# A graph layer with a highway gate: the root rows come by plain gathers and VectorE adds, and the last group of edges begins one product sooner

## The chip, the cores and the metric

The kernel runs on one core of a Trainium2 chip. Times are device microseconds. The core has five engines that run side by side, each in the order of its own instruction stream: TensorE (PE in the profile, its weight loads PEld), VectorE (DVE), ScalarE (ACT), GpSimd (POOL) and SyncE (SP). Large contiguous loads and stores are issued from SP; every gather and scatter by row indices is issued from POOL. Sixteen DMA engines carry out both.

## The reference

There are 1250 nodes with 1024 features in fp32, 20000 directed edges sorted by their destination, and 8 edge types. Cut to what matters:

```python
h = maximum(layernorm(x), 0)
u = h @ root + bias
for r in range(8):
    mask = (edge_type == r)
    sums = segment_sum(h[src] * mask[:, None], dst, 1250)
    cnt  = segment_sum(mask, dst, 1250)
    u = u + (sums / maximum(cnt, 1)[:, None]) @ weight[r]
z = concatenate([u, h], axis=1) @ w_gate + b_gate
out = x + tanh(u) * z + h * (1 - z)
```

## The kernel before

**The matrices.** The kernel multiplies h by ten 1024 x 1024 matrices and u by an eleventh, in fp32, numbered s: s = 0 to 7 are the eight edge types' weights, s = 8 is `root`, s = 9 (`LAST`) is the lower half of `w_gate` (for h), and s = 10 (`NM - 1`) is its upper half (for u). Products with s = 0 and s = 10 run over five pairs of 128-row blocks (`product`, seven batches of matmuls each, with a call `between(j)` after each batch). Products with s = 1 to 9 are cut by a fast scheme into seven smaller products n = 0 to 6 (function `kind`), written (s, n) here. Each (s, n) has five calls, `call(0)` to `call(4)`, at which work for the other engines is put into their streams; `at_call` holds where the program stands. In `kind`, L487 and L506 add a product's inner part (`ys`) in PSUM for the even and the odd blocks, `inner_sums` (L315 to L327) forms sums of quarters of the weights (the right sums) and of h (the left sums), and `to_rows_of` (L416 to L437) adds results into rows. `inner_sums` for the next product is emitted by `next_sums`, right after `call(2)`. Left sums that `LOADED` names for (s, n) are loaded from DRAM instead of made.

**The rows.** The products with s = 0 to 7 are stored as rows to `y[g]`, in three groups of edge types (g = 0, 1, 2, the types from `R0[g]` on), h times `root` to `hr_dram`, and s = 9 to `z_dram`.

**The edges.** While the products run, DVE and POOL build an index (`columns`, `positions`, `nodes_in_order`): for each group, nodes sorted by their number of edges, and for each node up to `SLOTS` rows of `y[g]` to add. This index work is a generator, one step at a call; the calls in `FULL_CALLS` get none, and the few small matmuls in it wait for a chosen call (`while at_call[2] != 2`).

`edges(g, to, late, more, lag, ring, seq)` then adds up a group. For each of the ten blocks of sorted nodes there is an accumulator u (128 x 1024). `first_u` reads it from `u_dram[g - 1]` by a gather (for g = 0 it is the bias). Then come `K[g][d]` slots: `slot_row` (L1446) gathers one row of `y[g]` for each of 128 nodes into the next of five buffers `got`, and `add_slot` (L1457) multiplies it by a weight and adds it to u on DVE. One slot is one step of the generator. For groups 0 and 1 the block is scattered to `u_dram[g]` behind its last slot (L777). For the last group (`LG`, g = 2) blocks come in the order `SEQ` and stay in SBUF as `us[d]`; there the rows of `hr_dram` are added as well, by `add_hr` (through `rows_of`, L766), an indirect DMA that adds what it gathers to u on the way: for the blocks from the third on, four steps ahead of the block's first slot, and for the first two (`HR_LATER`) after call (9, 0, 3). The accumulators of the fifth to the ninth block lie in parts of `h_all` that stage 9 no longer needs (`U_LATER`).

**Pacing.** `spread(e, total, of)` gives the steps of a group to the calls: each call of (s, n) counts `SHARE[n]` parts, each call of a gate product (s = 10) counts `GATE` parts, and after each call so many steps have been made as the counted parts ask for. Group 0 runs from (3, 1) to (6, 1), group 1 from there to (9, 0), and the last group from (9, 0) to the end of the third gate product; the borders are `CHANGE`. Between group 1 and the last group the program finishes the rows of the product before (`rest()`), stores what is held (`store_rows()`), and passes a branch on the register `far` (L1818) that is not taken here.

**The gate.** A gate product i uses blocks 2i and 2i + 1 of `SEQ`: their u is turned (`gate_turned`, transposes L571, copies L576, sums L609) and put through tanh (`gate_h`) during the product before, and z and h rows are gathered with an add (`gate_z`, `gate_d`).

Of the kernel before, what the change touches and what calls it, by code (L numbers as in the profile page):

```python
# [15 lines left out]
OP = mybir.AluOpType  # L16
# [5 lines left out]
def tile_rgcn_highway(  # L22
# [31 lines left out]
    nc = tc.nc  # L54
# [11 lines left out]
    ND = -(-N // P)  # L66
    NP = ND // 2
    NCH = 160
    FULL = E // NCH
    G = 3  # L70
    R0 = (0, 3, 6, R)
    K = ((21, 10, 8, 7, 7, 6, 5, 5, 4, 3), (21, 10, 8, 7, 7, 6, 5, 5, 4, 3),
         (17, 7, 6, 5, 4, 4, 3, 3, 2, 2))
    LAST = R + 1
    CALLS = 5
    BEGIN = (3, 1)
    WAIT1 = 3
    FULL_CALLS = [(4, k) for k in range(5)] + [(n, 3) for n in range(7)]
    CHANGE = ((6, 1), (9, 0))
    SEQ = (4, 5, 6, 7, 8, 9, 2, 3, 0, 1)  # L80
    REGULAR = {9: (5,)}
    LOADED = {7: (0, 1, 2, 3, 4, 5), 8: (0, 1, 2, 3, 4, 6), 9: (0, 2, 3, 4)}
    SHARE = (9, 11, 9, 11, 9, 11, 10)
    GATE = 15
    U_LATER = range(4, 9)
    HR_LATER = 2
    SLOTS = 22
    NCNT = SLOTS + 2
    STEP = 8
# [11 lines left out]
    GOT = 5  # L101
    UB = 4
    LATE = 4
# [8 lines left out]
    def nrows(d):  # L112
        return min(P, N - d * P)
# [13 lines left out]
    hr_dram = dram.tile([N, D], F32, name="hr_dram")  # L127
# [587 lines left out]
    NM = len(mats)  # L715
    fac = [Factors(w) for w in mats]

    at_call = [0, 0, 0]
# [98 lines left out]
    def nodes_in_order(pos, ids_f, room, many):  # L817

        parts = []
        for g in range(G):  # L820
            a, b, small = room(g)
            a = a[:, :KEYS].rearrange("p (c q) -> p c q", q=P)
            b = b[:, :2 * ND * ND].rearrange("p (c d) -> p c d", d=2 * ND)
            hi_i, lo, hi, block, lo_f = [small[:, k * ND:(k + 1) * ND] for k in range(5)]
            hi_i, lo, hi = hi_i.bitcast(I32), lo.bitcast(I16)[:, :ND], hi.bitcast(I16)[:, :ND]
            at = pos[:, g * ND:(g + 1) * ND]
            nc.vector.tensor_copy(block, many[:, :ND])
            nc.vector.tensor_copy(hi_i, at)
            nc.vector.tensor_single_scalar(hi_i, hi_i, 7, op=OP.arith_shift_right)
            nc.vector.tensor_copy(hi, hi_i)  # L830
            nc.vector.scalar_tensor_tensor(lo, hi_i, float(-P), at, op0=OP.mult, op1=OP.add)
            nc.vector.tensor_tensor(a, lo[:, :, None].to_broadcast([P, ND, P]),
                                    many[:, None, :].to_broadcast([P, ND, P]), op=OP.is_equal)
            yield
            nc.vector.tensor_tensor(b[:, :, :ND], hi[:, :, None].to_broadcast([P, ND, ND]),
                                    many[:, None, :ND].to_broadcast([P, ND, ND]), op=OP.is_equal)
            nc.vector.tensor_tensor(b[:, :, ND:], b[:, :, :ND],
                                    block[:, :, None].to_broadcast([P, ND, ND]), op=OP.mult)
            nc.vector.tensor_scalar(b[:, :, :ND], b[:, :, :ND], ids_f[:, :1], None, op0=OP.mult)
            parts.append((a, b, lo_f))  # L840
        while at_call[2] != 2:
            yield
        p = sum_bank("ps_q")[:, :2 * G * ND].rearrange("p (g d) -> p g d", g=G)
        for g, (a, b, lo_f) in enumerate(parts):
            for c in range(ND):
                nc.tensor.matmul(p[:, g], a[:, c], b[:, c], start=(c == 0), stop=(c == ND - 1))
        for g, (a, b, lo_f) in enumerate(parts):
            nc.vector.tensor_copy(lo_f, p[:, g, :ND])
            nc.vector.scalar_tensor_tensor(node[:, g, :], p[:, g, ND:], float(P), lo_f,
                                           op0=OP.mult, op1=OP.add)  # L850
            nc.vector.scalar_tensor_tensor(node_key[:, g, :], lo_f, float(ND), p[:, g, ND:],
                                           op0=OP.mult, op1=OP.add)
            if g:
                nc.vector.tensor_single_scalar(node_key[:, g, :], node_key[:, g, :], g * KEYS,
                                               op=OP.add)
        for g in range(G):
            for d in range(ND):
                rows_of(idx[:, g, d, :], table_rows, node_key[:, g, d:d + 1])
            yield
# [44 lines left out]
    def positions(runs, pos, ids_f, room):  # L904
# [50 lines left out]
        nc.vector.reduce_sum(first.rearrange("p g d -> p (g d)")[:, :, None],  # L955
                             pairs.rearrange("p g d e -> p (g d) e"), axis=AX.X)
        yield
        while at_call[2] != 2:
            yield
        p = sum_bank("ps_q")  # L960
        for k, t in enumerate((above, ones)):
# [30 lines left out]
    with ExitStack() as early:  # L992
# [20 lines left out]
        class Normed:  # L1013
# [13 lines left out]
            def spread(self):  # L1027
                n = self.n
                nc.vector.bn_aggr(self.mv[:n], self.st[:n].rearrange("p a b -> p (a b)"))
                nc.scalar.activation(self.sd[:n], self.mv[:n, 1:2], AF.Sqrt, bias=eps[:n])  # L1030
# [383 lines left out]
    with ExitStack() as edges_part:  # L1414
# [7 lines left out]
        def got():  # L1422
            t = gpool.tile([P, D], F32, name="got")
            if fresh[0]:
                nc.vector.memset(t, 0.0)
                fresh[0] -= 1
            return t
# [24 lines left out]
        def add_slot(u, g, d, k, at, w, t=None):  # L1452
            n = nrows(d)
            if t is None:
                t = slot_row(g, d, k, at)
            w = w[:n, d, k:k + 1]
            nc.vector.scalar_tensor_tensor(u[:n], t[:n], w, u[:n], op0=OP.mult, op1=OP.add)  # L1457

        us = {}

        def new_u(q, g=0):

# [12 lines left out]
                rows_of(u[:n], u_dram[g - 1][:, :], node[:n, g, d:d + 1])  # L1475
            return u

        def edges(g, to, late=0, more={}, lag=GOT, ring=True, seq=range(ND)):

            places = range(ND)
            starts = [late + sum(K[g][d] for d in seq[:q]) for q in range(ND + 1)]
            leaves = [starts[q + 1] - 1 + lag for q in places]
            reads = [max(-1, starts[q] - (9 if q in more else 5),
                         leaves[q - UB] if ring and q >= UB else -1,
                         starts[UB - 1] - 4 if not ring and q >= UB else -1) for q in places]
            u, then, early = {}, {}, []
            reads[0] = late - 3  # L1490
            for t in range(-1, leaves[-1] + 4):
                if 0 <= t < LATE:
                    early.append(slot_row(g, seq[0], t, idx[:, g]))
                for q, d in enumerate(seq):
                    if starts[q] <= t < starts[q + 1]:
                        add_slot(u[q], g, d, t - starts[q], idx[:, g], w_of[:, g],
                                 early.pop(0) if early else None)
                for q, d in enumerate(seq):
                    if t == leaves[q]:
                        then[t + 3] = to(q, d, u[q])  # L1500
                if then.get(t):
                    then[t]()
                for q, d in enumerate(seq):
                    if t == reads[q]:
                        u[q] = first_u(g, q, d)
                    if q in more and t == starts[q] - 4:
                        more[q](d, u[q])
                yield

        def u_back(g):  # L1510
# [25 lines left out]
        def kinds(first, end):  # L1536

            return [(a, b) for a in range(first[0], NM) for b in range(7 if a <= LAST else NP)
                    if first <= (a, b) < end]
# [269 lines left out]
        late = LATE  # L1809
# [35 lines left out]
                    p.next()  # L1845


        LG = G - 1
        def add_hr(d, u):
            n = nrows(d)  # L1850
            rows_of(u[:n], hr_dram[:, :], node[:n, LG, d:d + 1], OP.add)

        def place_of(what, i, part):

            o = ("z", "d").index(what)
# [106 lines left out]
                if i == NP - 1:  # L1962
                    gate_d(i)

        whole_u = []

        def keep_u(q, d, u):
            us[d] = u
            if q < HR_LATER:
                whole_u.append((d, u))  # L1970

        last = edges(LG, keep_u, LATE + 1, {q: add_hr for q in range(HR_LATER, ND)}, 4, False, SEQ)
        next(last)
        between = spread(last, LATE + 1 + sum(K[LG]) + 8, kinds((s, i), (NM - 1, NP - 2)))
        hooks = {(5, 0): load_bias, (6, 0): lambda: gate_bias(0), (5, 1): lambda: gate_h(0),
                 (5, 2): lambda: gate_turned(0, (0,)), (5, 3): lambda: gate_turned(0, (1,)),
                 }
        while s < NM - 1:
            def beside_h(k):
                between(k)  # L1980
                if whole_u and at_call >= [LAST, 0, 3]:
                    add_hr(*whole_u.pop(0))
                if s == LAST and (i, k) in hooks:
                    hooks[i, k]()

            step(s, i, beside_h)
            s, i = next(steps, (NM, 0))
# [107 lines left out]
```

## Time and profile before

| | |
|---|---|
| timed runs | 1267.61, 1269.86 and 1890.47 us, median 1269.86 |
| profiled execution | 1271.14 us, span 1269.3 us, granted TensorE clock 0.996 |
| PE busy | 1246.7 us, 98% of the span |
| DVE busy | 956.3 us, 75% |
| POOL busy | 465.1 us, 37% |
| DMA | 314.28 MB, mean 248 GB/s |

The profile's page describes one execution. The span runs from the first to the last instruction. Busy time of an engine leaves out its semaphores, branches and DMA issues, except that POOL's time for making an indirect DMA's descriptors counts. "Idle before, releaser" says how long the engine stood ahead of an instruction and what ended that; a wait for several things is put down to the one that came last. The DMA share is the mean busy share of the 16 DMA engines in a stretch; it can pass 1.0, since the time of a packet includes some overlap.

### The profile page before, as it was taken

What the parts mean: (1) busy time and instruction counts of PE and PEld (TensorE: products, weight loads), DVE (VectorE), ACT (ScalarE), POOL (GpSimd) and SP (SyncE); (2) the same over time, 40 slices, a digit from 0 to 9 for tenths busy, and PEclk for the clock granted to TensorE, in tenths of its full rate; (3) what the DMA queues carried; (4) which work ended last, traced back from release to release, by engine and by line L of the source; (5) the groups of instructions that cost most, each with busy time, mean ns of one, the idle gap of its engine ahead of it and who ended that gap; (6) DMA issues with size and microseconds to landing.
All of it is one profiled execution on the core that took longest, in us unless ns stands there. A gap on an engine that the chain in (4) does not pass through costs nothing. (4 is left out here: it accounts for less than half of the span.)

```text
span 1269.3 us, 13590 instructions
## 1 busy us (share of the span) xinstructions
PE 1246.7 (98%) x4787; PEld 895.5 (71%) x4787; DVE 956.3 (75%) x1142; ACT 274.5 (22%) x371; POOL 465.1 (37%) x404
## 2 busy tenths in 40 slices
PE   9999999999999999999999999999999997999997
PEld 5444677777777777777777777777777776674443
DVE  6545898884869788777877778888888785786864
ACT  3452211121121112112112111211211121212230
POOL 0330000007214345323423234453543266558752
PEclk9999999999999999999999999999999999999999
DMA  8965445834648898997987858699898899988885
GB/s 303 199 183 163 157 150 195 288 106 143 213 145 289 238 326 260 336 371 252 349 311 259 270 186 284 239 326 315 318 307 270 285 279 317 315 283 167 205 179 123
DMA packets 129387, 314.28 MB, mean 248 GB/s; under 512 B 30923, under 2 KB 32146, under 8 KB 129150
## 3 DMA queue, kind: packets, MB, share of 16 engines
q1 hardware_dynamic: 84462, 182.05, 43.3%
q0 software_dynamic: 44560, 130.77, 34.5%
q8 instruction: 38, 0.62, 0.2%
q10 hardware_dynamic: 288, 0.52, 0.1%
q14 instruction: 39, 0.32, 0.1%
HBM read 255.25 MB, written 90.18 MB: 272 GB/s over the span
## 5 line engine op out<-in xcount | busy, mean ns | idle before, releaser
L1446 POOL DMA_INDIRECT got<-y,idx x205 | 273.2, 1333 | 415.0 <-DVE u L1457 328.7
L373 PE MATMUL ps<-w,h_all 128*128 128x256 f32 x1104 | 258.9, 379 | 0.0
L373 PE MATMUL ps_n<-w,w 128*128 128x256 f32 x976 | 233.8, 383 | 8.0 <-DVE ps L487 6.5
L1457 DVE SCALAR_TENSOR_TENSOR u<-got,w_of,u 128x1024 f32<-128x1024 f32 (+1 forms) x173 | 221.0, 1279 | 15.8 <-DMA got<-y,idx 14.8
L373 PEld LDWEIGHTS ps<-w,h_all 128*128 128x128 f32 x1104 | 209.6, 190 | 29.3 <-issue 0.7
L373 PEld LDWEIGHTS ps_n<-w,w 128*128 128x128 f32 x976 | 186.3, 192 | 60.8 <-issue 26.6
L380 PE MATMUL ps_b<-w,h_all 128*128 128x512 f32 x504 | 226.6, 592 | 0.0
L380 PEld LDWEIGHTS ps_b<-w,h_all 128*128 128x128 f32 x504 | 95.8, 190 | 93.7 <-issue 90.4
L627 PE MATMUL ps_b<-w,h_all 128*128 128x512 f32 x312 | 139.1, 592 | 0.2 <-ACT h_all L578 0.2
L373 PE MATMUL ps_q<-w,w 128*128 128x256 f32 x488 | 115.7, 380 | 3.0 <-DVE w L320 2.8
L373 PE MATMUL ps<-w,w 128*128 128x256 f32 x488 | 116.0, 381 | 0.0
L373 PE MATMUL ps_n<-w,h_all 128*128 128x256 f32 x488 | 115.3, 379 | 0.0
L496 ACT COPY ps<-ps_n 128x1024 f32<-128x1024 f32 x61 | 60.8, 997 | 250.4 <-PE ps_n L373 239.9
L627 PEld LDWEIGHTS ps_b<-w,h_all 128*128 128x128 f32 x312 | 58.8, 190 | 71.8 <-issue 70.3
L320 DVE TENSOR_TENSOR w<-w 128x1024 f32<-128x1024 f32 x61 | 74.4, 1220 | 44.9 <-PE ps_n L373 42.7
L487 DVE TENSOR_TENSOR ps<-ps_n,inner 128x512 f32<-128x512 f32 x61 | 42.6, 698 | 82.3 <-PE ps L373 82.1
L373 PEld LDWEIGHTS ps_q<-w,w 128*128 128x128 f32 x488 | 92.4, 190 | 16.9 <-DVE w L320 3.6
L373 PEld LDWEIGHTS ps<-w,w 128*128 128x128 f32 x488 | 93.4, 191 | 13.0
L373 PEld LDWEIGHTS ps_n<-w,h_all 128*128 128x128 f32 x488 | 92.7, 190 | 13.0 <-issue 0.5
L474 ACT COPY ps<-ps_n 128x512 f32<-128x512 f32 x61 | 34.8, 570 | 245.8 <-PE ps_n L373 178.6
L276 DVE TENSOR_TENSOR w<-w,w 128x2048 f32<-128x2048 f32 x36 | 82.2, 2285 | 0.3
L627 PE MATMUL ps<-w,h_all 128*128 128x512 f32 (+1 forms) x136 | 57.6, 568 | 0.0
(249 smaller groups left out, 1111.0 us busy)
## 6 DMA issues: line engine op xcount, KB each, us to landing
w<-lefts_dram SPq DMA_DIRECT2D x102, 512.0 KB
w<-in_L_gnn_weight_dram SPq DMA_DIRECT2D x31, 1024.0 KB
y<-row SPq DMA_DIRECT2D x84, 256.0 KB
y<-w SPq DMA_DIRECT2D x42, 256.0 KB
w<-in_L_gnn_w_gate_dram SPq DMA_DIRECT2D x8, 1024.0 KB
lefts_dram<-w SPq DMA_DIRECT2D x14, 512.0 KB
h_dram<-h_all SPq DMA_DIRECT2D x9, 512.0 KB
y<-row SPq DMA_DIRECT2D x9, 512.0 KB
```

The source lines that it names most:

```text
L276: nc.vector.tensor_sub(w[to], w[a], w[b])
L320: nc.vector.tensor_sub(rights[:, :2].rearrange("p a (k n) -> p a k n", k=2), w[:, :, H:].rearrange("p (a k) n -> p a k n", a=2), w[:, 0:2] ...
L373: nc.tensor.matmul(p, a[:, k], b[:, k], start=(fresh and k == 0), stop=(k == a.shape[1] - 1), skip_group_check=True)
L380: nc.tensor.matmul(to, h_op[NP - 1][:, ORDER[n], k], w[:, k], start=(fresh and k == 0), stop=(k == KQ - 1), skip_group_check=True)
L474: nc.scalar.copy(even[:, 0], x)
L487: nc.vector.tensor_add(even[:, 1], x, ys)
L496: nc.scalar.copy(odd, x[:, None, :].to_broadcast([P, 2, Q]))
L627: nc.tensor.matmul(b[:, at], aop[:, i, k, :], w.of[i][:, k, at], start=(fresh and k == 0), stop=(k == KQ - 1), skip_group_check=True)
L1446: nc.gpsimd.indirect_dma_start(out=t[:n], out_offset=None, in_=y[g][:, :], in_offset=bass.IndirectOffsetOnAxis(ap=at[:n, d, k:k + 1], axis=0),
L1457: nc.vector.scalar_tensor_tensor(u[:n], t[:n], w, u[:n], op0=OP.mult, op1=OP.add)
```

## The change

Five things are changed.

- Rows of `hr_dram` are no longer added by the DMA. Each block of the last group gets one more step (`HR`), at which `hr_row` gathers the rows plainly into a `got` buffer and DVE adds them to u. The step stands after the block's slots; the first block's stands after the second's.
- The last group begins at (8, 6) instead of (9, 0), so group 1 ends there too; u of a block is read five steps ahead, and the tail of empty steps at the end is gone.
- `GATE` is 12 instead of 15; the last group has 68 steps instead of 66.
- `LOADED`: the left sums of (8, 5) are loaded and those of (8, 6) are made, where it was the other way about.
- Index steps leave out call 2 of each product instead of call 3, and the index's small matmuls wait for call 3 instead of call 2.

```diff
-    FULL_CALLS = [(4, k) for k in range(5)] + [(n, 3) for n in range(7)]
-    CHANGE = ((6, 1), (9, 0))
+    FULL_CALLS = [(4, k) for k in range(5)] + [(n, 2) for n in range(7)]
+    CHANGE = ((6, 1), (8, 6))
...
-    LOADED = {7: (0, 1, 2, 3, 4, 5), 8: (0, 1, 2, 3, 4, 6), 9: (0, 2, 3, 4)}
+    LOADED = {7: (0, 1, 2, 3, 4, 5), 8: (0, 1, 2, 3, 4, 5), 9: (0, 2, 3, 4)}
...
-    GATE = 15
+    GATE = 12
...
-    HR_LATER = 2
...
-        while at_call[2] != 2:          # in nodes_in_order and in positions
+        while at_call[2] != 3:
...
-        def edges(g, to, late=0, more={}, lag=GOT, ring=True, seq=range(ND)):
-            places = range(ND)
-            starts = [late + sum(K[g][d] for d in seq[:q]) for q in range(ND + 1)]
-            leaves = [starts[q + 1] - 1 + lag for q in places]
-            reads = [max(-1, starts[q] - (9 if q in more else 5),
-                         leaves[q - UB] if ring and q >= UB else -1,
-                         starts[UB - 1] - 4 if not ring and q >= UB else -1) for q in places]
+        def hr_row(d):
+            n = nrows(d)
+            t = got()
+            rows_of(t[:n], hr_dram[:, :], node[:n, LG, d:d + 1])
+            return t
+
+        def edges(g, to, late=0, seq=range(ND)):
+            places, end, work = range(ND), g == LG, []
+            for q, d in enumerate(seq):
+                work += [(q, k) for k in range(K[g][d])]
+                if end and q:
+                    work += [(q, HR)] + [(0, HR)] * (q == 1)
+            starts = [late + work.index((q, 0)) for q in places]
+            leaves = [late + max(j for j, w in enumerate(work) if w[0] == q) + GOT * (not end)
+                      for q in places]
+            reads = [max(-1, starts[q] - 5, leaves[q - UB] if q >= UB and not end else -1)
+                     for q in places]
...
-                for q, d in enumerate(seq):
-                    if starts[q] <= t < starts[q + 1]:
-                        add_slot(u[q], g, d, t - starts[q], idx[:, g], w_of[:, g],
+                if 0 <= t - late < len(work):
+                    q, k = work[t - late]
+                    d = seq[q]
+                    if k == HR:
+                        h, n = hr_row(d), nrows(d)
+                        nc.vector.tensor_add(u[q][:n], u[q][:n], h[:n])
+                    else:
+                        add_slot(u[q], g, d, k, idx[:, g], w_of[:, g],
                                  early.pop(0) if early else None)
...
-                    if q in more and t == starts[q] - 4:
-                        more[q](d, u[q])
...
-        def add_hr(d, u):
-            n = nrows(d)
-            rows_of(u[:n], hr_dram[:, :], node[:n, LG, d:d + 1], OP.add)
...
-        last = edges(LG, keep_u, LATE + 1, {q: add_hr for q in range(HR_LATER, ND)}, 4, False, SEQ)
+        last = edges(LG, keep_u, LATE + 1, SEQ)
         next(last)
-        between = spread(last, LATE + 1 + sum(K[LG]) + 8, kinds((s, i), (NM - 1, NP - 2)))
+        between = spread(last, LATE + 1 + sum(K[LG]) + ND, kinds((s, i), (NM - 1, NP - 2)))
...
             def beside_h(k):
                 between(k)
-                if whole_u and at_call >= [LAST, 0, 3]:
-                    add_hr(*whole_u.pop(0))
```

More of the change, by code (lines that the diff above doesn't have):

```diff
@@ L957, in positions @@
         yield
-        while at_call[2] != 2:
+        while at_call[2] != 3:
             yield
@@ L1459, in tile_rgcn_highway @@
         us = {}
+        LG, HR = G - 1, -1
         def new_u(q, g=0):
@@ L1476, in first_u @@
             return u
-        def edges(g, to, late=0, more={}, lag=GOT, ring=True, seq=range(ND)):
-            places = range(ND)
-            starts = [late + sum(K[g][d] for d in seq[:q]) for q in range(ND + 1)]
-            leaves = [starts[q + 1] - 1 + lag for q in places]
-            reads = [max(-1, starts[q] - (9 if q in more else 5),
-                         leaves[q - UB] if ring and q >= UB else -1,
-                         starts[UB - 1] - 4 if not ring and q >= UB else -1) for q in places]
+        def hr_row(d):
[14 more added lines that the diff above has]
+                     for q in places]
             u, then, early = {}, {}, []
             reads[0] = late - 3
-            for t in range(-1, leaves[-1] + 4):
+            for t in range(-1, leaves[-1] + 4 - 3 * end):
                 if 0 <= t < LATE:
                     early.append(slot_row(g, seq[0], t, idx[:, g]))
-                for q, d in enumerate(seq):
-                    if starts[q] <= t < starts[q + 1]:
-                        add_slot(u[q], g, d, t - starts[q], idx[:, g], w_of[:, g],
+                if 0 <= t - late < len(work):
[6 more added lines that the diff above has]
+                        add_slot(u[q], g, d, k, idx[:, g], w_of[:, g],
                                  early.pop(0) if early else None)
@@ L1845, in tile_rgcn_highway @@
                     p.next()
-        LG = G - 1
-        def add_hr(d, u):
-            n = nrows(d)
-            rows_of(u[:n], hr_dram[:, :], node[:n, LG, d:d + 1], OP.add)
         def place_of(what, i, part):
@@ L1963, in gate_u @@
                     gate_d(i)
-        whole_u = []
         def keep_u(q, d, u):
             us[d] = u
-            if q < HR_LATER:
-                whole_u.append((d, u))
-        last = edges(LG, keep_u, LATE + 1, {q: add_hr for q in range(HR_LATER, ND)}, 4, False, SEQ)
+        last = edges(LG, keep_u, LATE + 1, SEQ)
         next(last)
-        between = spread(last, LATE + 1 + sum(K[LG]) + 8, kinds((s, i), (NM - 1, NP - 2)))
+        between = spread(last, LATE + 1 + sum(K[LG]) + ND, kinds((s, i), (NM - 1, NP - 2)))
         hooks = {(5, 0): load_bias, (6, 0): lambda: gate_bias(0), (5, 1): lambda: gate_h(0),
```

## The prediction

> **What bounds the kernel now.** First the page, for the engine that fills the span, then what this engine waited for.
>
> ```profile
> span 1269.3 us, 13590 instructions
> PE 1246.7 (98%) x4787; PEld 895.5 (71%) x4787; DVE 956.3 (75%) x1142; ACT 274.5 (22%) x371; POOL 465.1 (37%) x404
> ```
> ```profile
> PE ps_n L373 <- DVE ps L487: 6.5, 2, 4.6
> PE ps_q L373 <- DVE w L320: 2.8, 2, 2.5
> PE ps_n L373 <- ACT ps L474: 1.6, 3, 0.5
> ...
> PE ps_n L627 <- DVE h_all L609: 0.6, 1, 0.6
> PE ps_q L373 <- DVE w L326: 0.2, 1, 0.2
> ```
>
> TensorE (PE) is the bound. The matmuls are the same before and after, so all that can be won is PE's 22.6 us without work and the matmuls that ran slowly. The second view (columns: total, times, longest) names few waits, the two largest on VectorE (DVE). The table by stretches of 10 us shows where (after the length: PE, PEld, DVE, ACT, POOL busy, granted clock, DMA share, GB/s):
>
> ```profile
> 1050.00:1060.00 10.00, 10.00 (x46) 8.44 (x45) 3.72 (x4) 1.16 (x2) 8.17 (x7) 1.00 1.03 357
> 1060.00:1070.00 10.00, 5.42 (x13) 3.10 (x12) 6.01 (x7) 0.58 (x1) 7.54 (x5) 0.85 1.06 321
> 1070.00:1080.00 10.00, 7.50 (x35) 6.22 (x33) 5.36 (x5) 1.00 (x1) 4.25 (x4) 0.98 1.05 286
> 1080.00:1090.00 10.00, 7.58 (x27) 4.55 (x25) 6.97 (x8) 1.07 (x2) 2.48 (x3) 1.00 0.94 290
> 1090.00:1100.00 10.00, 10.00 (x32) 7.16 (x33) 7.63 (x8) 4.39 (x4) 7.91 (x6) 0.83 0.90 250
> ```
>
> One hole, 1060 to 1100, with DMA full. Its price comes from PE's timeline (start, duration):
>
> ```profile
> 1007.21 1.89 PE L373 MATMUL ps_q<-w,w 128*128 128x256 f32 x8
> 1012.39 3.60 PE L380 MATMUL ps_b<-w,h_all 128*128 128x512 f32 x8
> 1015.82 1.89 PE L373 MATMUL ps_n<-w,w 128*128 128x256 f32 x8
> 1017.55 1.89 PE L373 MATMUL ps<-w,w 128*128 128x256 f32 x8
> ...
> 1053.77 1.89 PE L373 MATMUL ps_q<-w,w 128*128 128x256 f32 x8
> ...
> 1067.12 3.56 PE L373 MATMUL ps_n<-w,w 128*128 128x256 f32 x8 [4.58 <-DVE ps L487]
> 1078.36 1.99 PE L373 MATMUL ps_q<-w,w 128*128 128x256 f32 x8 [2.50 <-DVE w L320]
> 1084.45 3.60 PE L380 MATMUL ps_b<-w,h_all 128*128 128x512 f32 x8
> 1089.93 2.96 PE L373 MATMUL ps_n<-w,w 128*128 128x256 f32 x8 [1.88 <-DVE ps L487]
> 1096.90 3.60 PE L380 MATMUL ps_b<-w,h_all 128*128 128x512 f32 x8
> ```
>
> From 1007.21 to 1053.77 lie three products, 15.52 us each. In each, ps_b follows ps_q by 1012.39 - 1007.21 = 5.18 us, so product (9,4) should have had its ps_b at 1053.77 + 15.52 + 5.18 = 1074.47. It came at 1084.45, 9.98 late. From there to the next product are one ps_b batch (1015.82 - 1012.39 = 3.43) and three batches of 1.73 (1017.55 - 1015.82), 8.62 in all; the next started at 1096.90, 12.45 later, 3.83 too long. **The hole costs 13.8 us**; the waits named in it are 9.5, the rest is slow matmuls (3.56 and 2.96 us where 1.89 is usual, at a granted clock of 0.85 and 0.83).
>
> The Trainium skill, "TensorE: Matmul & The Clock Gate", Part 1, says the clock drops after an idle window of about 3.4 us. The wait of 4.58 us agrees; the wait of 1.88 us is shorter and was followed by slow matmuls all the same. By the page a leftover wait of 2 us would cost 2 us; by these rows up to 4. I go by the rows.
>
> Why was DVE late? The chain of waits (start, length) and DVE's timeline:
>
> ```profile
> 1039.82 12.15 DMA h_all<-u_dram,node
> 1053.43 14.86 DMA h_all<-hr_dram,node
> 1069.04 18.91 DMA got<-y,idx
> ```
> ```profile
> 1059.12 1.28 DVE L1457 SCALAR_TENSOR_TENSOR u<-got,w_of,u 128x1024 f32<-128x1024 f32 x1 [6.25 <-DMA got<-y,idx]
> ...
> 1066.38 0.69 DVE L487 TENSOR_TENSOR ps<-ps_n,inner 128x512 f32<-128x512 f32 x1
> ```
>
> DVE stood 6.25 us at a slot's multiply-add whose gathered rows had not come. Behind it in DVE's order were L506, L425, L315 and then L487, for which PE waited. The gathers were late because the accumulating gathers of hr_dram and the reads of u_dram sat in front of them.
>
> **The change part by part.**
>
> *Accumulating gathers go.* Ten gathers with an add become ten plain gathers into the ring `got`, and ten DVE adds. Rows (times to landing at the end; then the table's stretch without a hole):
>
> ```profile
> got<-y,idx POOLq DMA_INDIRECT x205, 7.3
> u<-hr_dram,node POOLq DMA_INDIRECT x5, 13.2
> h_all<-hr_dram,node POOLq DMA_INDIRECT x5, 13.9
> ```
> ```profile
> 800.00:989.96 189.96, 189.96 (x787) 149.13 (x786) 158.88 (x157) 37.86 (x51) 81.34 (x71) 1.00 0.87 298
> ```
>
> Plain ones land in 7.3 us, accumulating ones in 13 to 14, about 1.9 times as long. No row separates queueing from the transfer, so the relief is bounded: nothing (same bytes, the wait was the queue's) up to half of the time of each. I take most of it, because 0.87 DMA share over 190 us went without one PE wait, and the hole stood at 0.90 to 1.06. A second relief: before, a block's slots wait for the u read and then for the accumulate onto it (12.15 and 14.86 us in a row); after, only for the read. An hr gather now comes late in its block.
>
> *The DVE adds.*
>
> ```profile
> L1457 DVE SCALAR_TENSOR_TENSOR u<-got,w_of,u 128x1024 f32<-128x1024 f32 (+1 forms) x173 | 221.0, 1279 | 15.8 <-DMA got<-y,idx 14.8
> L320 DVE TENSOR_TENSOR w<-w 128x1024 f32<-128x1024 f32 x61 | 74.4, 1220 | 44.9 <-PE ps_n L373 42.7
> ```
>
> An add of this shape takes 1.22 us: 10 x 1.22 = 12.2 us of DVE, over about twelve products' time. DVE is not the bound there (3.7 to 7.6 of 10 us busy in the hole), so the cover is its own idle time; without it, 12.2 us would be the price.
>
> The Trainium skill, "SBUF — State Buffer", practical consequences under the port section, says that a DVE instruction with two SBUF inputs contends with GpSimd (POOL) instructions that read SBUF. If each add held POOL once, POOL would issue up to 12 us later in all; if descriptor writing is spared, as the page infers, nothing. No row here separates the two, and I add nothing.
>
> *Pacing.* Before, 66 steps are spread over 350 + 3 x 7 x 15 = 665 parts: 4.96 steps a product of 50 parts and 10.4 a gate product of 105. After, 5 + 53 + 10 = 68 steps over 50 + 350 + 3 x 7 x 12 = 652 parts: 5.21 and 8.76. The hr steps are now among them, so DMAs a product do not rise in stage 9 and fall at the gate. Group 1 pays: its 81 steps go into 955 parts instead of 1005, 4.24 a product instead of 4.03, 0.2 x 1.28 = 0.3 us of DVE per 15.5 us, where DVE is 158.88 / 189.96 = 84% busy. That is cover enough; else 0.3 x 19 = 5 us.
>
> *The boundary moves to (8,6),* with its flush of stores and the branch.
>
> ```profile
> 1010.81 1.06 POOL L1446 DMA_INDIRECT got<-y,idx  x1 [9.19 <-DMA hr_dram<-w]
> ```
>
> POOL waited 9.19 us there for stores; PE did not stop. After, queued behind POOL's wait are the four early slot gathers, whose first user is six steps away, more than a product. The stores of hr rows from (8,6) itself now come behind it on SP, and the first hr gather, step 13, falls in (9,1) (5.2 steps in (8,6), 9.9 by the end of (9,0), 15.6 by that of (9,1)), a product after those stores. No cost. At (8,6) the left sums are made (four 512-wide operations, 0.69 us each by the L487 row, 2.8 us) and at (8,5) loaded instead: a swap.
>
> *Index steps* leave the call ahead of the right sums and go to the one behind. The waits outside the hole that this may touch are L474 1.6 - 0.5, L320 2.8 - 2.5 and L326 0.2: 1.6 us. They may go, or as many new ones come; I take -0.5 between -1.6 and +1.6.
>
> *The gate products.*
>
> ```profile
> 1158.90:1184.70 25.80, 25.80 (x74) 12.33 (x73) 17.63 (x20) 7.23 (x10) 21.76 (x17) 1.00 0.81 145
> 1211.00:1236.90 25.90, 25.90 (x73) 12.34 (x72) 14.97 (x23) 7.33 (x10) 12.65 (x11) 1.00 0.85 178
> ```
> ```profile
> 1176.36 1.28 DVE L1457 SCALAR_TENSOR_TENSOR h_all<-got,w_of,h_all 128x1024 f32<-128x1024 f32 x1 [5.93 <-DMA got<-y,idx]
> 1179.64 2.60 DVE L1457 SCALAR_TENSOR_TENSOR h_all<-got,w_of,h_all 128x1024 f32<-128x1024 f32 x2 [1.99 <-DMA got<-y,idx]
> ```
>
> Without slots a gate product has at most 15.0 us of DVE (the second stretch, leftovers included); 8.76 steps of about 1.25 add 11.0: 26.0, just its length, against 28.0 before with 10.4 steps. The waits for `got` (5.93 + 1.99) come on top and made PE lose 0.6. After, the rate is lower but lasts through the third gate product. I take the 0.6 back and keep it as part of the leftover.
>
> **Sum**, against the profiled execution's 1271.14 us (span 1269.3): -13.8 (hole), -0.6 (gate), -0.5 (index), + 2.5 leftover waits with their slow matmuls (bounds 0 and 7, half the hole): 1258.7. The three timed runs have their median at 1269.86, 1.3 below the profiled one, so **1257.5 us**.
>
> **The rivals.**
>
> *Half the hole stays,* because what starved DVE was the number of gathers and u reads, not the kind. For it: the u read of 12.15 us is plain and as slow, and u reads stay. Against: they stand five steps ahead of their block now instead of nine, one at a time. It gives 1257.5 + 7 - 2.5 = 1262.
>
> *The change does not do what it says:* the hole stays whole, because POOL still holds one in-order queue and the ring of five. 1257.5 + 13.8 - 2.5 = 1269. Against it: the accumulate and its chain are named in the chain of waits.
>
> *Slower: the gate products' DVE overruns.* Place: (10,0) to (10,2), where the steps now reach to the last call. Each has 26.0 us of DVE work; if each also waits for `got` by twice the 7.9 us seen, it overruns by 15.9, 48 in three; the overrun of 28.0 + 7.9 - 25.8 = 10 was carried with 0.6 lost, so some 30 to 38 reach PE: 1257.5 + 34 = 1291. It decides once the waits pass about 7.3 us in all three (three overruns of 7.5 less the 10 carried are the 12.4 us forecast). For it: one product waited 7.9 us already, and the z and h gathers still accumulate in the same queue. Against: 15.0 us is too much for the work without slots, since that stretch holds leftovers; five steps now last 5 x 25.8 / 8.76 = 14.7 us instead of 12.4, so the ring covers a wait of 2.3 us more; and the other gate products need not wait as long.
>
> **How the numbers follow.** Forecast 0.64, half hole 0.18, whole hole 0.10, slower 0.08. The range: 1252.5 (13.8 + 0.6 + 1.6 = 16.0 won leaves 1254, less 1.5 for the runs' scatter) to 1266 (half hole with one more small wait); outside lie most of the last two cases. About 2% is what a measurement here can tell from no change, 25 us; no case wins that, the hole being 13.8, and only the slower one at its full price approaches it: faster 0.01, same 0.95, slower 0.04.
>
> **What would show it.** Right: PE busy 10 of 10 between 1050 and 1100 and no wait of PE on L487 or L320 there; ps_q every 15.52 us through (9,4); DMA share under 1.0 in stage 9; hr gathers landing in about 7 us; adds of 1.22 us. Wrong: a PE wait on L609 of several us in the gate products, a hole of the old kind in stage 9, a new one near the moved boundary, or PE waits before 300 us longer than 1.6.

## The result, and the profile after

The changed kernel takes 1255.77 us in the median of six runs (1255.32 to 1256.75); the kernel before, also with six runs, 1267.96. One of its six runs took 1890.47 us and is left out of the ratio; the median of the other five is 1267.61. The ratio is 0.9906, with a 95% interval of 0.9892 to 0.9919: 0.9% faster, inside the 2% bound, and clear of the scatter. The profiled execution took 1255.77 us, its span is 1254.0, 15.3 less than the profiled one before.

The page after, for PE, and PE's waits (total, times, longest). Line numbers behind the edit moved by one: L486 was L487, L372 was L373, L608 was L609, L1456 was L1457.

```profile
span 1254.0 us, 13612 instructions
PE 1242.1 (99%) x4787; PEld 895.5 (71%) x4787; DVE 967.4 (77%) x1152; ACT 275.0 (22%) x371; POOL 462.5 (37%) x404
```
```profile
PE ps_n L186 <- POOL eps L749: 1.4, 1, 1.4
PE ps L570 <- DVE h_all L1043: 1.2, 1, 1.2
PE ps_n L372 <- DVE ps L486: 0.8, 2, 0.5
PE ps_q L372 <- DVE w L325: 0.3, 1, 0.3
PE ps_b L626 <- ACT h_all L577: 0.2, 1, 0.2
```

PE stands idle 1254.0 - 1242.1 = 11.9 us instead of 22.6, which is 10.7 less, and is busy 4.6 us less with the same 4787 matmuls: those that ran slowly behind the waits are gone. Together this is the 15.3 us. The waits on L487 (6.5) and on L609 (0.6) have no successor; L320's fell from 2.8 to none. What is left is nearly all at the start of the program and at its end.

The same stretches of 10 us as before (length, PE, PEld, DVE, ACT, POOL, clock, DMA share, GB/s), and PE's ps_q batches through stage 9:

```profile
1050.00:1060.00 10.00, 10.00 (x45) 8.24 (x44) 9.56 (x11) 1.16 (x2) 6.09 (x5) 1.00 1.02 364
1060.00:1070.00 10.00, 10.00 (x43) 7.88 (x42) 7.48 (x8) 2.15 (x3) 4.33 (x3) 1.00 0.95 284
1070.00:1080.00 10.00, 10.00 (x40) 7.33 (x39) 7.12 (x8) 1.20 (x2) 5.87 (x6) 1.00 0.98 360
1080.00:1090.00 10.00, 10.00 (x40) 7.30 (x40) 8.75 (x9) 3.78 (x4) 4.82 (x4) 1.00 0.90 265
1090.00:1100.00 10.00, 10.00 (x56) 8.93 (x55) 7.81 (x7) 2.17 (x4) 7.24 (x6) 1.00 1.02 396
```
```profile
1037.80 1.89 PE L372 MATMUL ps_q<-w,w 128*128 128x256 f32 x8
1053.32 1.89 PE L372 MATMUL ps_q<-w,w 128*128 128x256 f32 x8
1068.84 1.89 PE L372 MATMUL ps_q<-w,w 128*128 128x256 f32 x8
```

PE is busy in all of them at full clock, and ps_q comes every 15.52 us through (9,4). DVE does more work there (7.1 to 9.6 of 10 us against 3.7 to 7.6) and it does it on time. The DMA share is hardly lower than in the hole. The DMA table (last number: us from issue to landing) and the groups of DVE:

```profile
got<-hr_dram,node POOLq DMA_INDIRECT x10, 7.5
h_all<-u_dram,node POOLq DMA_INDIRECT x5, 8.4
```
```profile
L1510 DVE TENSOR_TENSOR u<-u,got 128x1024 f32<-128x1024 f32 x5 | 6.1, 1218 | 0.0
```

The plain hr gathers land in 7.5 us instead of 13 to 14, the reads of u into h_all in 8.4 instead of 12.3, and an add takes 1.22 us.

### The profile page after: what moved, and what is told of

Read it like the earlier page. It is cut to its first block, busy times and chain, and to the rows that moved or that the text cites. A ratio compares the mean times of both kernels' runs of the same rounds, so it can differ in the third digit from the quotient of the medians.

```text
span 1254.0 us, 13612 instructions
## 1 busy us (share of the span) xinstructions
PE 1242.1 (99%) x4787; PEld 895.5 (71%) x4787; DVE 967.4 (77%) x1152; ACT 275.0 (22%) x371; POOL 462.5 (37%) x404
## 4 chain that ended last, share of the span: by engine, by line
PE 86%; DVE 5%; issue 4%; POOL 2%; DMA 2%; POOLq 0%; ACT 0%; SPq 0%; DVEq 0%
PE ps L372 25%; PE ps_n L372 23%; PE ps_b L379 16%; PE ps_q L372 8%; PE ps_b L626 7%; PE ps L626 4%; PE ps_n L626 1%; POOL out_dram L776 1%; POOL h_all L765 1%; DMA u<-u_dram,node 1%; DVE w L275 1%; DMA h_all<-out_dram,node 1%; DVE u L1456 0%; POOL got L1445 0%; PE ps L570 0%
## 5 line engine op out<-in xcount | busy, mean ns | idle before, releaser
L1445 POOL DMA_INDIRECT got<-y,idx x205 | 277.7, 1355 | 392.0 <-DVE u L1456 310.3
L372 PE MATMUL ps<-w,h_all 128*128 128x256 f32 x1104 | 259.1, 379 | 0.0
L372 PE MATMUL ps_n<-w,w 128*128 128x256 f32 x976 | 230.9, 380 | 0.8 <-DVE ps L486 0.8
L372 PEld LDWEIGHTS ps<-w,h_all 128*128 128x128 f32 x1104 | 209.8, 190 | 28.8 <-issue 0.7
L1456 DVE SCALAR_TENSOR_TENSOR u<-got,w_of,u 128x1024 f32<-128x1024 f32 (+1 forms) x173 | 221.2, 1280 | 10.0 <-DMA got<-y,idx 6.1
L372 PEld LDWEIGHTS ps_n<-w,w 128*128 128x128 f32 x976 | 185.5, 190 | 52.6 <-issue 28.0
L372 PE MATMUL ps_q<-w,w 128*128 128x256 f32 x488 | 115.4, 379 | 0.3 <-DVE w L325 0.3
L372 PE MATMUL ps_n<-w,h_all 128*128 128x256 f32 x488 | 115.3, 379 | 0.0
L372 PE MATMUL ps<-w,w 128*128 128x256 f32 x488 | 115.3, 379 | 0.0
L372 PEld LDWEIGHTS ps_q<-w,w 128*128 128x128 f32 x488 | 92.8, 190 | 13.3 <-DVE w L325 0.7
L372 PEld LDWEIGHTS ps_n<-w,h_all 128*128 128x128 f32 x488 | 92.9, 190 | 12.9 <-issue 0.5
L372 PEld LDWEIGHTS ps<-w,w 128*128 128x128 f32 x488 | 92.9, 190 | 12.5
L486 DVE TENSOR_TENSOR ps<-ps_n,inner 128x512 f32<-128x512 f32 x61 | 42.6, 698 | 70.1 <-PE ps L372 69.8
```

Source lines behind the costliest of these rows:

```text
L372: nc.tensor.matmul(p, a[:, k], b[:, k], start=(fresh and k == 0), stop=(k == a.shape[1] - 1), skip_group_check=True)
L486: nc.vector.tensor_add(even[:, 1], x, ys)
L1445: nc.gpsimd.indirect_dma_start(out=t[:n], out_offset=None, in_=y[g][:, :], in_offset=bass.IndirectOffsetOnAxis(ap=at[:n, d, k:k + 1], axis=0),
```

## The experiments

Two questions: what made the hole in stage 9 (the adding on the way, the chain of read, accumulate and slots, the number of gathers, the pacing), and which parts of the change carry the gain. Ratios are to the kernel before, timed beside each run, with 95% intervals.

**Plain gathers alone.** From the changed kernel, with start, `LOADED`, GATE and index steps put back.

```diff
-    FULL_CALLS = [(4, k) for k in range(5)] + [(n, 2) for n in range(7)]
-    CHANGE = ((6, 1), (8, 6))
+    FULL_CALLS = [(4, k) for k in range(5)] + [(n, 3) for n in range(7)]
+    CHANGE = ((6, 1), (9, 0))
...
-    GATE = 12
+    GATE = 15
...
```

> The changed kernel with the old start (9, 0), the old GATE of 15, the old LOADED and the old place of the index steps: only the plain gathers with VectorE adds (and the u reads that go with them) are new. Theory, the accumulating gathers made the hole: PE waits in stage 9 under 2 us, 1254 to 1259 us. Rival, the late start and the pacing made it: PE waits of 6 us or more stay in stage 9, 1263 to 1269 us.

Measured 1268.76 us, ratio 0.9997 (0.9979 to 1.0015): no gain at all. Both theories fail. There is no PE wait in stage 9, as the first said, and yet the time is the rival's. PE's timeline in the gate, and DVE's rows there that waited for a gather:

```profile
1207.97 6.26 PE L626 MATMUL ps_n<-w,h_all 128*128 128x512 f32 x8 [7.42 <-DVE h_all L608]
```
```profile
1137.59 1.23 DVE L1510 TENSOR_TENSOR h_all<-h_all,got 128x1024 f32<-128x1024 f32 x1 [3.26 <-DMA got<-hr_dram,node]
...
1165.31 3.93 DVE L1456 SCALAR_TENSOR_TENSOR h_all<-got,w_of,h_all 128x1024 f32<-128x1024 f32 x3 [6.43 <-DMA got<-y,idx]
...
1197.62 1.23 DVE L1510 TENSOR_TENSOR h_all<-h_all,got 128x1024 f32<-128x1024 f32 x1 [8.39 <-DMA got<-hr_dram,node]
```

The loss moved from stage 9 to the gate. DVE waits 3.3, 6.4 and 8.4 us in three gate products, its left sums for the next product (L608) come late, and PE loses 7.42 us and 6.26 - 3.60 = 2.7 more in slow matmuls.

**The same with GATE 12,** the only difference to the last run.

```diff
-GATE = 15
+GATE = 12
```

> The run with plain gathers alone (old start, old index calls) with GATE 12 instead of 15 as its only difference. Theory: plain gathers and the slower rate in the gate are both needed and are enough together: no wait on the left sums (L608's line) in the gate, 1256 to 1259 us. Rival: the index calls or the earlier start carry the gain: 1264 us or more.

Measured 1259.85 us, 0.9921 (0.9905 to 0.9938), with no PE wait in stage 9 or in the gate. As the theory said, if a little above its upper end. GATE is worth about 9 us here.

**GATE 12 alone,** in the kernel before.

```diff
-    GATE = 15
+    GATE = 12
```

> The kernel before with GATE 12 alone: 66 steps over 602 parts, 5.5 a product in stage 9 and 9.2 a gate product. Theory, pacing helps only once the gathers are plain: the hole in stage 9 stays or grows, 1268 to 1276 us. Rival, pacing is the whole gain: under 1262 us.

Measured 1274.79 us, 1.0038 (1.0017 to 1.0060). PE's waits in stage 9:

```profile
PE ps_n L373 <- DVE ps L487: 6.6, 2, 5.3
PE ps_q L373 <- DVE w L320: 3.3, 1, 3.3
```

The hole stays, a little larger than the 9.5 us before. So of the two parts one gains nothing, the other costs 0.4%, and both together gain 0.8%.

**The late start,** in the changed kernel.

```diff
-    CHANGE = ((6, 1), (8, 6))
+    CHANGE = ((6, 1), (9, 0))
...
-    LOADED = {7: (0, 1, 2, 3, 4, 5), 8: (0, 1, 2, 3, 4, 5), 9: (0, 2, 3, 4)}
+    LOADED = {7: (0, 1, 2, 3, 4, 5), 8: (0, 1, 2, 3, 4, 6), 9: (0, 2, 3, 4)}
```

> The changed kernel with the last group begun at (9, 0) again and the old LOADED, GATE staying at 12 (68 steps over 602 parts, 5.6 a product). Theory: the earlier start is not needed once the gathers are plain: 1255 to 1258 us. Rival: the earlier start carries part of the gain, because the same steps now crowd stage 9: 1259 to 1265 us with waits of PE on VectorE there.

Measured 1256.89 us, 0.9910 (0.9893 to 0.9926), no PE wait in stage 9 or the gate. The earlier start is worth 1 us or nothing as long as GATE is 12.

**GATE 15 with the early start.**

```diff
-    GATE = 12
+    GATE = 15
```

> The changed kernel with GATE 15 again, begun at (8, 6): 68 steps over 715 parts, 10.0 a gate product instead of 8.8. Theory, the rate of steps in the gate products decides: a PE wait on the left sums (the line of L608) of 3 to 8 us in the gate, 1260 to 1268 us. Rival, the earlier start saves it: 1255 to 1258 us.

Measured 1259.89 us, 0.9926 (0.9900 to 0.9952). PE's waits in the gate:

```profile
PE ps_n L626 <- DVE h_all L608: 1.8, 1, 1.8
PE ps L570 <- DVE u L1510: 0.6, 1, 0.6
```

Between the two forecasts: the wait is there but short. An earlier start and a lower GATE both leave fewer steps to the gate products, and the changed kernel has both: 105 parts of 715 with 68 steps are 10.0 a product here, 84 of 652 are 8.8 in the changed kernel, and 105 of 665 are 10.7 in the run with plain gathers alone. That the early start helps by this, and not by placing the steps differently within a product, is argued and was not tried by itself.

**The gate's own gathers made plain,** in the run with plain gathers alone, GATE 15.

```diff
-    rows_of(place_of("z", i, part)[:n], z_dram[:, :], node[:n, LG, d:d + 1], OP.add)
+    rows_of(place_of("z", i, part)[:n], z_dram[:, :], node[:n, LG, d:d + 1])
     (and the same for "d" and h_dram)
```

> The run with plain gathers alone (old start, GATE 15), with the gate's own z and h gathers turned into plain ones that overwrite: the gate bias and tanh(u) are left out of the rows they should be added to. Theory A, those accumulating gathers make VectorE wait for slot rows in the gate: waits of VectorE on gathers there fall from 15 us to under 6, the PE wait of 7.4 us on the left sums goes, 1255 to 1259 us. Theory B, the sheer VectorE work of 10.3 steps a gate product makes it: 5 us or more of that wait stay, 1264 us or more.

Measured 1256.80 us, 0.9897 (0.9880 to 0.9913), no PE wait in the gate. DVE's rows there that waited for a gather:

```profile
1158.30 3.93 DVE L1456 SCALAR_TENSOR_TENSOR h_all<-got,w_of,h_all 128x1024 f32<-128x1024 f32 x3 [1.89 <-DMA got<-y,idx]
...
1185.88 1.23 DVE L1510 TENSOR_TENSOR h_all<-h_all,got 128x1024 f32<-128x1024 f32 x1 [3.66 <-DMA got<-hr_dram,node]
```

5.6 us of waits instead of 18.1, with the same steps (10.7 a product) and GATE 15; the 15 us and the 10.3 steps in the expectation were too low. The gathers themselves got quicker: those of h land in 5.7 us (into `h_all`) and 6.0 us (into `w`) in the median, against 8.6 and 9.8 with the adding. Theory A holds: what starves DVE in the gate is the accumulating gathers of z and h ahead of the slots' gathers, and not the DVE work.

**A high rate that ends early,** to see whether the steps in the third gate product were the trouble.

```diff
-between = spread(last, LATE + 1 + sum(K[LG]) + ND, ...)
+between = spread(last, LATE + 1 + sum(K[LG]) + ND + 8, ...)
```

> The run with plain gathers alone (old start, GATE 15, old index calls), with eight empty steps at the end as before the change: 76 steps over 665 parts, 12 a gate product, the last real one in the first half of the third gate product. If the rate of steps made its wait of 7.4 us on the left sums: a longer one, 1269 us or more. If it was that steps now reach to the end of the third gate product, behind its four accumulating gathers: a wait under 2 us, under 1260 us.

Measured 1267.32 us, 0.9990 (0.9976 to 1.0004). PE's timeline:

```profile
1179.39 3.70 PE L626 MATMUL ps_n<-w,h_all 128*128 128x512 f32 x8 [3.15 <-DVE h_all L608]
...
1210.68 5.84 PE L626 MATMUL ps_n<-w,h_all 128*128 128x512 f32 x8 [5.24 <-DVE h_all L608]
```

The wait is a little longer in all (8.4 us against 7.42) and now falls at two products. So the reach into the third product does not explain it: the wait stays where the steps end sooner. That a higher rate costs more is not shown: the time is under the 1269 us written for it, and not longer than the 1268.76 us of the run with plain gathers alone. Nor does the rate act by itself, since at 10.7 steps and without the gate's accumulating gathers there was no wait.

**Only the adding taken away,** in the kernel before.

```diff
-            rows_of(u[:n], hr_dram[:, :], node[:n, LG, d:d + 1], OP.add)
+            rows_of(u[:n], hr_dram[:, :], node[:n, LG, d:d + 1])
```

> The kernel before, with the ten hr gathers in their old places and onto the same accumulators, but as plain gathers that overwrite: the sums of the earlier groups are left out of u. Order, chain (read, gather, slots), bytes and pacing stay; only the adding on the way is gone. Theory A, the adding transfer itself made the hole: PE waits between 1050 and 1100 us fall under 3 us, 1254 to 1260 us. Theory B, the chain of read, gather, slots or the mere number of gathers made it: at least 6 us of PE waits stay there, 1263 to 1269 us.

Measured 1262.29 us, 0.9939 (0.9919 to 0.9958): half way, and neither theory. PE's timeline in the hole, and POOL's queue (packets, MB, share of 16 engines) over 1005 to 1118 us, first the kernel before, then this run:

```profile
1074.82 1.99 PE L373 MATMUL ps_q<-w,w 128*128 128x256 f32 x8 [2.44 <-DVE w L320]
1077.36 1.99 PE L373 MATMUL ps_n<-w,w 128*128 128x256 f32 x8 [0.54 <-ACT ps L474]
1086.09 1.99 PE L373 MATMUL ps_n<-w,w 128*128 128x256 f32 x8 [1.57 <-DVE ps L487]
```
```profile
q0 software_dynamic: 6569, 22.03, 66.2%
```
```profile
q0 software_dynamic: 6822, 22.73, 57.9%
```

Of 9.5 us of waits 4.6 stay, and the matmuls behind them are no longer slow. With a few more bytes the queue takes 57.9% of 113 us instead of 66.2%. The difference is 9.4 us of all 16 engines for the nine hr gathers in that stretch, by this estimate about 1 us each.

**The chain taken away too:** plain gathers in the old places, into the ring.

```diff
-            rows_of(u[:n], hr_dram[:, :], node[:n, LG, d:d + 1], OP.add)
+            rows_of(got()[:n], hr_dram[:, :], node[:n, LG, d:d + 1])
```

> The kernel before, with the ten hr gathers plain, in their old places, and into the ring of got buffers, where nobody reads them: h times root is left out of u, and no slot waits for them. Against the run with plain gathers onto the accumulators only the chain is gone. Theory A, the chain read, gather, slots made the 4.5 us of PE waits left there: under 1.5 us between 1050 and 1100, 1255 to 1259 us. Theory B, the number of gathers and u reads did: 3 us or more stay, 1260 us or more.

Measured 1266.35 us, 0.9974 (0.9960 to 0.9988). PE's waits in stage 9, and POOL's two waits for an unread gather (1000 to 1118 us):

```profile
PE ps_n L373 <- DVE ps L487: 4.4, 2, 4.0
PE ps_b L380 <- DVE w L396: 0.8, 1, 0.8
```
```profile
POOL got L1446 <- DMA got<-hr_dram,node: 24.9, 6, 7.4
POOL got L766 <- DMA got<-hr_dram,node: 3.5, 1, 3.5
```

The number is theory B's: 5.2 us of waits stay without the chain. But the unread gathers each take one of the five ring buffers, and before POOL can fill such a buffer again it waits for the gather to land, 28.4 us in all, which the kernel before does not do. So the edit put a new delay in front of the slots' gathers, and the run settles nothing about the chain.

**A shorter lead of the u reads,** in the kernel before.

```diff
-            reads = [max(-1, starts[q] - (9 if q in more else 5),
+            reads = [max(-1, starts[q] - 5,
```

> The kernel before with u read five steps ahead of a block instead of nine, the accumulating gather one step behind it as before at four. Theory, the chain of read, accumulate, slots is what is short of time: a shorter lead makes the hole larger, PE waits of 10 us or more in stage 9, 1270 to 1280 us. Rival, early reads crowd the queue and the spread-out reads of the changed kernel are part of its gain: a smaller hole, 1258 to 1266 us.

Measured 1278.80 us, 1.0071 (1.0054 to 1.0087). PE's waits in stage 9, PE's timeline at two of them, and POOL's waits for the reads of u (1000 to 1118 us):

```profile
PE ps_n L373 <- DVE ps L487: 11.4, 2, 8.3
PE ps_q L373 <- DVE w L320: 2.3, 1, 2.3
```
```profile
1067.25 3.78 PE L373 MATMUL ps_n<-w,w 128*128 128x256 f32 x8 [3.04 <-DVE ps L487]
1079.70 3.34 PE L373 MATMUL ps_q<-w,w 128*128 128x256 f32 x8 [2.27 <-DVE w L320]
```
```profile
POOL h_all L766 <- DMA h_all<-u_dram,node: 22.0, 4, 8.1
POOL u L766 <- DMA u<-u_dram,node: 4.6, 1, 4.6
```

13.7 us of waits, as the theory said: with accumulating gathers one step behind the reads the chain is short of time, and spreading the reads is no gain in itself. But it is short in its own way. POOL stands 26.6 us at the accumulating gathers until the read has landed, and every gather behind waits with it; in the kernel before POOL hardly stands there. The accumulating gathers, issued late, landed in 6.5 and 7.0 us in the median, as fast as plain ones.

**Accumulating gathers behind the slots,** in the changed kernel: no slot waits for them, the hr steps are empty.

```diff
-            for t in range(-1, leaves[-1] + 4 - 3 * end):
+            for t in range(-1, leaves[-1] + 4 - 3 * end + GOT * end):
...
-                        h, n = hr_row(d), nrows(d)
-                        nc.vector.tensor_add(u[q][:n], u[q][:n], h[:n])
+                        pass
...
+                    if end and t == leaves[q] + GOT:
+                        n = nrows(d)
+                        rows_of(u[q][:n], hr_dram[:, :], node[:n, LG, d:d + 1], OP.add)
```

> The changed kernel with the hr rows again added by the DMA, but five steps behind the block's last slot, so that no slot waits for it; the hr steps stay in the pacing and are empty. Theory A, the accumulating transfer itself slows the queue behind it: gathers land in 9 us or more in stage 9 and a hole of 4 to 10 us comes back, 1259 to 1266 us. Theory B, what mattered was the chain read, accumulate, slots: no PE wait on L487's like, 1254 to 1257 us.

Measured 1270.01 us, 0.9992 (0.9971 to 1.0012), the whole gain lost. PE's timeline; the load that PE waited for, from the chain of waits (start, time to landing); and DVE's waits for the DMA between 1000 and 1118 us, in this run and then, for slot rows, in the kernel before:

```profile
1073.10 3.75 PE L372 MATMUL ps_q<-w,w 128*128 128x256 f32 x8 [3.83 <-DMA w<-lefts_dram]
```
```profile
1057.24 15.72 DMA w<-lefts_dram
```
```profile
DVE u L1456 <- DMA u<-u_dram,node: 3.3, 1, 3.3
```
```profile
DVE u L1457 <- DMA got<-y,idx: 14.8, 5, 6.2
DVE h_all L1457 <- DMA got<-y,idx: 5.2, 3, 2.3
```

SP's issues of these loads in the changed kernel:

```profile
1056.97 8.93 SPq L336 DMA_DIRECT2D w<-lefts_dram  x2
```

Stage 9 has a hole again, at another place: PE waits for left sums that SP loads. The load took 15.72 us. In the changed kernel SP issued it at 1056.97, and ps_q began at 1068.84 without a wait, so there it landed within 11.87 us. (The 8.93 us of SP's row run from the first of two issues to the end of the second and are no transfer time.) That fits one half of theory A, the transfer slows what shares the engines with it. The other half fails: DVE does not wait for one slot row here, where it waited 20.0 us in the kernel before, and the slots' gathers land in 8.4 us in the median, not 9 or more. As theory B has it, no PE wait falls on the successor of L487 in stage 9, yet the time is not B's. The load is not the whole of the loss: the last block's accumulate comes so late that the chain at the end of the program also grew (span less the start of the last matmuls 1270.2 - 1251.3 = 18.9 us against 1254.0 - 1242.4 = 11.6 in the changed kernel). The edit made that itself.

**The index steps put back,** in the changed kernel.

```diff
-    FULL_CALLS = [(4, k) for k in range(5)] + [(n, 2) for n in range(7)]
+    FULL_CALLS = [(4, k) for k in range(5)] + [(n, 3) for n in range(7)]
...
-        while at_call[2] != 3:
+        while at_call[2] != 2:
```

> The changed kernel with the index steps back out of call 3 and in call 2. Theory: the index steps are worth what the prediction took for them, -0.5 us, so this is 1256.3 us with PE waits of about 1.6 us between 100 and 300 us. Rival: they are worth nothing or cost, 1255 us or less, with as much waiting in either place.

Measured 1257.61 us, 0.9914 (0.9894 to 0.9934) against 0.9906 (0.9892 to 0.9919) of the changed kernel: not told apart. PE's waits there:

```profile
PE ps_n L372 <- ACT ps L473: 1.0, 2, 0.5
PE ps_q L372 <- DVE w L319: 0.3, 1, 0.3
PE ps_q L372 <- DVE w L325: 0.2, 1, 0.2
```

1.5 us instead of the 0.8 us on L486 that the changed kernel has early: the changed kernel waits 0.7 us less, too little for these runs to show in the time.

## Why the prediction was right, and where not

- **The hole, -13.8 us: right.** It is gone whole, and plain gathers with VectorE adds take it away (plain gathers alone: no PE wait in stage 9). Why was only half seen. The adding on the way is about half (waits 9.5 to 4.6 us with nothing else changed). The other half is not settled. That no slot waits behind an accumulate any more fits the run with accumulating gathers behind the slots, where DVE waited for no slot row, but that run has the new pacing too. The shorter lead and the unread gathers in the ring each gave POOL a new wait (26.6 and 28.4 us), so neither shows what the chain cost in the kernel before. What plain gathers alone also change is that u is read five steps ahead, and that hr gathers are steps of the pacing and no longer come on top of it; neither was tried by itself with plain gathers.
- **The landing times: read too strongly.** The prediction set 13 to 14 us against 7.3 and took most of the difference as relief. In the run with the shorter lead accumulating gathers landed in 6.5 and 7.0 us, so the 13 to 14 us were not the adding alone. Where only the adding was taken away, in the gate, 8.6 and 9.8 us became 5.7 and 6.0.
- **The leftover, +2.5 us: too large, and the fit of the sum is in part luck.** 0.3 us of waits was left in stage 9. Without this term the sum wins 14.9 us, and the two profiled executions lie 15.4 apart (1271.14 and 1255.77). But the profiled execution before was 3.5 us above the 1267.61 of its kernel, and the sum took off only 1.3 for that, since 1269.86 was the middle of three runs of which one took 1890.47. The forecast was thus 12.4 us below a base of 1269.86, and the measured time is 11.8 us below 1267.61: the base was 2.3 us too high, more than the 1.7 us by which 1257.5 lies above 1255.77, and 11.8 us is less than the hole of the profiled execution alone.
- **Pacing: the step that was weighed wrongly.** The prediction counted GATE 12 as relief worth 0.6 us with its cover in place. The runs show that the gain hangs on the pacing: with GATE 15 and the old start the plain gathers gain nothing, with GATE 12 or with the early start 0.7 to 0.8%. The sum came out right because both were in the change, but it did not say that the plain gathers are worthless without either.
- **The slower rival: its mechanism is real.** VectorE starved by z and h gathers in the gate, PE late on the left sums: this is the run with plain gathers alone, at waits of 3.3, 6.4 and 8.4 us. It was put at "once the waits pass about 7.3 us in all three"; 18.1 us in all cost PE 10. The term behind that point was too high: DVE's work in a gate product was taken as 26.0 us with 8.8 steps, and a stretch of 26 us inside the changed kernel's gate holds 19.5 (the table's row below; DVE also stands some of that time). What spared it is fewer steps a product; DVE still waits up to 6.1 us for slot rows there (the row below it), and PE does not notice.

```profile
1163.00:1189.00 26.00, 26.00 (x74) 12.53 (x73) 19.48 (x24) 7.33 (x10) 21.66 (x18) 1.00 0.93 222
```
```profile
1183.81 2.61 DVE L1456 SCALAR_TENSOR_TENSOR u<-got,w_of,u 128x1024 f32<-128x1024 f32 x2 [6.14 <-DMA got<-y,idx]
```

- **The adds, the boundary, group 1: right.** 1.22 us an add, hidden; POOL waits 6.99 us for stores at the border and PE does not; no PE wait in group 1. The Trainium skill, "SBUF — State Buffer", practical consequences, says that a VectorE instruction with two SBUF inputs contends with a GpSimd instruction that reads SBUF; this was left out of the sum. POOL's gathers of slot rows take 1355 ns in the mean instead of 1333, 4.5 us more over 205 of them, and POOL's busy time is 462.5 us instead of 465.1, so nothing like 12 us shows.
- **Index steps, -0.5 us: of the right size** by the waits (0.7), not settled by the times.
- **The sign for a full queue: wrong.** A DMA share under 1.0 in stage 9 was to show the forecast right; it is 1.02 in two stretches without a hole. So the share alone does not tell whether an engine waits.
- **Slow matmuls: not settled.** By the rows before, a leftover wait of 2 us was to cost up to 4. In the run with only the adding taken away, waits of 2.44, 0.54 and 1.57 us were each followed by matmuls of 1.99 us, nearly the usual 1.89. The longer waits of 7.42 and 3.83 us were followed by 6.26 (3.60 is usual) and 3.75 (1.89 is usual). So far this is as the Trainium skill, "TensorE: Matmul & The Clock Gate", Part 1, has it, with its window of about 3.4 us. But beside the 1.88 us of the kernel before, two more waits under 3.4 us were followed by slow matmuls: 3.04 and 2.27 us in the run with the shorter lead, by 3.78 and 3.34. The length of a single wait does not decide it in these runs, and what does stays open.

## What to carry to other kernels

A gather that adds on the way can delay what shares its queue. Here VectorE had idle time, and a plain gather and an add were cheaper; the place to look was who waits behind the gather, not how full the DMA is. When a wait is taken out of one stage, look at the pacing of the next one with the same streams: here the whole gain reappeared as a loss in the gate until the steps were spread anew, so a change of work and a change of schedule have to be tried together as well as apart. A part that gains nothing alone may still be necessary. And an experiment that takes one wait away should be looked through for a wait that it brings in: two runs here answered less than they seemed to, because POOL stood somewhere new.

## What the runs showed of the hardware that was not expected

By an estimate from two stretches of 113 us, an accumulating gather of 512 KB takes about 1 us more of all 16 engines than a plain one (9.4 us for nine). In the gate, the gathers of h landed in 8.6 and 9.8 us with the adding and in 5.7 and 6.0 us without; yet in the run with the shorter lead accumulating gathers landed in 6.5 and 7.0 us. With such gathers behind the slots, a load that SP issued took 15.72 us, where the same load landed within 11.87 us beside plain gathers; that the one caused the other was not tried by itself. DMA shares of 0.90 to 1.06 went with the hole in one kernel, and of 0.90 to 1.02 with none in the other.
